# First products in a new order with filler matmuls, some normalizing work on GpSimd, and one layer norm cut in two

## The chip, the cores and the metric

The kernel is one program on one core of a Trainium2 chip. The metric is the device time of that core in microseconds (us), the median of several executions. Five engines run side by side, each through its own list of instructions in order: TensorE (PE in the profile, with its weight loads as PEld), VectorE (DVE), ScalarE (ACT), GpSimd (POOL) and SyncE (SP), which here only issues transfers. GpSimd issues transfers too, through a queue of its own. Engines wait for each other by semaphores.

## The reference

Two batches of 512 tokens with 512 features (x) go through three residual stages, each behind a layer norm without weights:

```python
x = x + xattn(layernorm(x), ctx, ctx, mask)   # 16 heads of 32; 8192 context tokens per batch
x = x + window_attn(layernorm(x))             # 16 heads, a window of 7 keys, latent projection
x = x + ffn(layernorm(x))                     # 16 experts, 128 tokens each, and a shared part
```

The first stage computes `q = ln(x) @ Wq.T + bq`, `k = ctx @ Wk.T + bk`, `v = ctx @ Wv.T + bv`, then `softmax(q k / sqrt(32)) v` with a mask over the 8192 keys, and `@ Wo.T + bo`. Everything is in float32, with the exception of small bfloat16 helpers (mask rows, subtracted maxima). The change touches the start of this stage and its end, where its projection meets the layer norm of the second stage.

## The kernel before

**Stage 1.** A unit is a batch and a group of four heads (8 units), a chunk is 512 context columns (16 per unit). The main loop goes over slots, one chunk per slot. In a slot the keys of the next chunk are projected (`project_k` and `keys_in`, products of L278), maxima of the scores are taken (`max_part`), and, 18 slots later, scores, exponentials and values of the same chunk are made. In the first 17 slots `max_part` runs four times per slot: four products with the mask row (L319), eight instructions of query times keys (L325), and two reductions on VectorE straight out of PSUM (L330). Its PSUM tiles come from a pool of three (`pairs`), two per call: the second tile of call 1 is the first tile of call 0 again, and has to wait until call 0's first reduction has read it. The queries of other head groups and of batch 1 are spread over these slots as single pieces (`later`), one behind each `max_part`. Batch 1's share of them is `query_norm` (its statistics) and four `query_in` (normalize 128 tokens, turn them on TensorE).

**Before the loop** stands `first_products`. SyncE issues the transfers in this order: token chunks 0 and 1 (128 tokens, 256 KB each, L70), the first 128 columns of Wq and of Wk (256 KB each, L168), the first context chunk in two halves (512 KB each, L484), token chunks 2 and 3, the four token chunks of batch 1 (1 MB, L63), the second context chunk (1 MB, L245), the rest of Wq (768 KB). GpSimd issues the mask and three bias vectors. `mask_rows` makes an additive mask (`mbias`, L209, on VectorE), spreads it over `junk` (L212, GpSimd), multiplies it with an identity to get the mask row of the first chunk (L218, copied by ScalarE, L222), and turns it whole (L226) so that GpSimd can write it to DRAM (L229, L233), from where later slots read their mask rows. `tokens_in` does statistics (L84, L85), square root (L88, ScalarE), reciprocal (L90), normalization (L94), four transposes (L502) and one copy back (L503, ScalarE) for one token chunk. After two of these come the first 256 queries (L192), then the keys of the first context chunk in halves (L278), then token chunks 2 and 3. The order on each engine is made by a scheduler that works with its own estimate of times; ScalarE's list there is: square roots of chunks 0 and 1, copy of chunk 0, square root of chunk 2, copy of chunk 1, mask row, square root of chunk 3, queries, keys.

**End of stage 1.** After the last slot eight `proj_residual` calls (L111 to L115) multiply by Wo and add to x, first four for batch 0, then four for batch 1. After the second one `finish_last` divides the last unit by its sums (reciprocal of 128x512, L458, then L462 and L463). After the fourth one `layernorm_stats` is called for batch 0, and behind each of the last four a chunk of batch 0 is normalized and turned (L606); the second stage begins with the products of L698, which wait for the copies of those four.

Of the kernel before, what the change touches and what calls it, by code (L numbers as in the profile page):

```python
# [19 lines left out]
P = 128  # L20
# [23 lines left out]
def perceiver_kernel(  # L44
# [45 lines left out]
        nc.vector.reciprocal(rs[:, these], sd[:, these])  # L90
        return mv, rs

    def normalized(dst, n, mv, rs):
        nc.vector.tensor_scalar(  # L94
            dst, x_sb[:, n, :], mv[:, n, 0:1], rs[:, n : n + 1], ALU.subtract, ALU.mult
        )

# [27 lines left out]
    with ExitStack() as es:  # L125
# [17 lines left out]
            return t  # L143

        mask_i = cp.tile([P, B, S2 // P], I32, name="mask_i")
        nc.gpsimd.dma_start(out=mask_i, in_=mask)
        bq_c = cp.tile([P, G], F32, name="bq_c")
        nc.gpsimd.dma_start(out=bq_c, in_=bq)
        bk_c = cp.tile([P, G], F32, name="bk_c")
        nc.gpsimd.dma_start(out=bk_c, in_=bk)  # L150
        bv_c = cp.tile([P, G], F32, name="bv_c")
        nc.gpsimd.dma_start(out=bv_c, in_=bv.rearrange("(g p) -> p g", p=P))
        ones32 = cp.tile([P, DK], F32, name="ones32")
        nc.vector.memset(ones32, 1.0)

# [6 lines left out]
        junk = cp.tile([P, KC], BF16, name="junk")  # L162
# [16 lines left out]

        def query_in(b, c):  # L180
            xn = tmp.tile([P, D], F32, tag="row", name="xn")
            normalized(xn, b * (NT // B) + c, *ln[b])
            transposed(xnT[b][:, :, ts(c, P)], xn, ps_q)

        pq = {}
# [20 lines left out]
        def mask_rows():  # L206


            nc.vector.tensor_scalar(mbias, mask_i, 0.0, -BIG, ALU.is_equal, ALU.mult)  # L209

            cols = junk.rearrange("p (c m) -> p c m", m=P)
            nc.gpsimd.tensor_scalar(  # L212
                cols, mbias[:, 0, 0 : KC // P].unsqueeze(2).to_broadcast([P, KC // P, P]),
                -1.0, None, ALU.mult,
            )
            tp = ps.tile([P, KC], F32, tag="ps", name="tpk")
            for c in range(KC // P):
                nc.tensor.matmul(  # L218
                    tp[:, ts(c, P)], lhsT=cols[:, c, :], rhs=ident_h, start=True, stop=True
                )  # L220
            mk_t[0] = mp.tile([P, KC], BF16, tag="mkh", name="mk", bufs=3)
            nc.scalar.copy(mk_t[0], tp)  # L222

            tp = ps.tile([P, B, P], F32, tag="ps", name="tpk")
            for b in range(B):
                nc.tensor.transpose(tp[0 : S2 // P, b, :], mbias[:, b, :], ident)  # L226
            mh = tmp.tile([S2 // P, P], BF16, name="mh")
            nc.vector.tensor_scalar(mh, tp[0 : S2 // P, 0, :], -1.0, None, ALU.mult)
            nc.gpsimd.dma_start(out=mrow_h, in_=mh)  # L229
# [246 lines left out]


        def first_products():
            load_cols(wq_sb, wq, slice(0, P))
            load_cols(wk_sb, wk, slice(0, P))  # L480
            ctx_t[0, 0] = ctxp.tile([P, DC, KC], F32, tag="ctx", name="ctx_t")
            for half in range(2):
                hs = ts(half, KC // 2)
                nc.sync.dma_start(  # L484
                    out=ctx_t[0, 0][:, :, hs],
                    in_=ctxT[0, :, hs].rearrange("(c p) s -> p c s", p=P),
                )
            load_chunks((2, 3))
            load_x(1)
            mask_rows()  # L490
            xnT[0] = pp.tile([P, DC, S], F32, tag="p", name="xnT")
            xn = pp.tile([P, NT // B, D], F32, tag="p", name="xn4")
            k_t[0] = kp.tile([P, KC], F32, tag="k", name="kt")

            def pair():
                return pairs.tile([P, 2, KC], F32, name="sx2")[:, 0, :]

            def tokens_in(c, tp):
                normalized(xn[:, c, :], c, *layernorm_stats(tmp, range(c, c + 1)))
                tp = tp.rearrange("p (n k) -> p n k", n=4)  # L500
                for i in range(4):
                    nc.tensor.transpose(tp[:, i, :], xn[:, c, ts(i, P)], ident)  # L502
                nc.scalar.copy(xnT[0][:, :, ts(c, P)], tp)  # L503
# [24 lines left out]
        def later_w(slot, dst, src, first):  # L528
# [1 line left out]
            load_cols(dst, src, slice(first, D))  # L530

        rest_in = {
            0: lambda: load_cols(wq_sb, wq, slice(P, D)),
            4: lambda: later_w(4, wk_sb, wk, P), 6: lambda: later_w(6, wv_sb, wv, 0),
        }
        wv_sb = cp.tile([P, DC, D], F32, name="wv_sb")
# [2 lines left out]
        for slot in range(NS + LAG):  # L539
            if slot == LAG:  # L540
                first_ps.close()
                ps = ps_q = ctx.enter_context(tc.tile_pool(name="a_ps", bufs=8, space=PSUM))
            if slot + 1 < NS + NKC:
                load(slot + 1)
            elif slot + 1 == NS + NKC:
                wo_sb = load_w(wo, ctxp, "ctx")
                wqkv_t = [load_w(wqkv[:, ts(i, D)], ctxp, "ctx") for i in range(3)]
            if slot + 1 < NS:
# [39 lines left out]
                    max_finish(u, i)  # L588


        turned_b0 = []
        for n in range(NT):
            if n == 1:
                values(*waiting)
            proj_residual(qT, wo_sb, None, n, ps, tmp)
            if n == 1:
                finish_last()
            m = n - NT // B
            if m == -1:
                ln_b0 = layernorm_stats(lnp, range(NT // B))  # L600
            if m >= 0:
                xn = tmp.tile([P, D], F32, tag="row", name="xn")
                normalized(xn, m, *ln_b0)
                tp = ps.tile([P, 4, P], F32, tag="ps", name="tp")
                for c in range(4):
                    nc.tensor.transpose(tp[:, c, :], xn[:, ts(c, P)], ident)  # L606
# [32 lines left out]
    with ExitStack() as es:  # L639
# [215 lines left out]
                )  # L855
            return pf

        lns, pairs = {"b0": ln_b0}, []
# [274 lines left out]
```

## Time and profile before

| what | value |
|---|---|
| median of 3 runs | 3671.01 us (3670.76 to 3671.19) |
| the profiled execution, its own time | 3670.19 us |
| its span in the trace | 3667.8 us |
| granted TensorE clock | 1.00 |
| TensorE busy | 3642.3 us, 99% of the span |
| VectorE, ScalarE, GpSimd busy | 2179.6, 1696.4, 2170.0 us |
| TensorE's first instruction | 7.41 us after the start of the span |
| first `max_part` begins | 25.65 us |
| end of stage 1's projections | about 2629 us |

A line of the timeline has the start in us, the busy time in us, the engine, the source line and operation, output<-inputs, shape and count; in square brackets is the idle time of the engine before it and what ended that. A line of the waits has the waiting engine and line, what it waited for, and the total, the count and the longest wait. The lines themselves stand in the prediction.

### The profile page before, as it was taken

The page shows a single profiled execution, that of the slowest core. Times are in us where ns is not written, and L with a number is a line of the kernel's source. Part 1 is how long each engine was busy: PE and PEld are TensorE (multiplying, and loading weights), DVE is VectorE, ACT ScalarE, POOL GpSimd, SP SyncE. Part 2 cuts the span into 40 slices and gives each one's busy share as a digit, 9 for nine tenths or more (in the row PEclk, how much of TensorE's full clock was granted, in tenths as well). Part 3 has the DMA queues.
Part 4 walks back from the last instruction along what each step waited for, and adds up shares of the span by engine and source line. Part 5 has one row for each costly group of instructions (what it writes and reads, how often), then busy time and mean ns, then how long its engine had stood idle before and what let it go on. Part 6 is the DMA issues. An engine that isn't in the chain of part 4 may idle for free.

```text
span 3667.8 us, 108951 instructions
## 1 busy us (share of the span) xinstructions
PE 3642.3 (99%) x47460; PEld 2057.9 (56%) x47460; DVE 2179.6 (59%) x5260; ACT 1696.4 (46%) x3417; POOL 2170.0 (59%) x653
## 2 busy tenths in 40 slices
PE   8999999999999999999999999999999999999999
PEld 4554555555455555545555555544455468888777
DVE  7976677677767766766776676789654711111111
ACT  2245555555555555555555555588554111111110
POOL 0059989998998999899899899921322000000000
PEclk9999999999999999999999999999999999999999
DMA  6322221221223443221222222122201068998886
GB/s 205 107 73 66 74 72 61 74 74 60 74 74 105 127 124 96 72 74 63 70 74 66 67 74 68 59 85 92 93 7 70 35 228 304 317 322 313 313 310 207
DMA packets 147757, 444.47 MB, mean 121 GB/s; under 512 B 9648, under 2 KB 14800, under 8 KB 121680
## 3 DMA queue, kind: packets, MB, share of 16 engines
q1 hardware_dynamic: 142224, 426.02, 34.5%
q0 software_dynamic: 5056, 11.50, 1.2%
q8 instruction: 372, 6.09, 0.7%
q14 instruction: 105, 0.86, 0.1%
HBM read 428.75 MB, written 8.73 MB: 119 GB/s over the span
## 4 chain that ended last, share of the span: by engine, by line
PE 97%; issue 1%; DMA 1%; POOL 1%; DVE 0%; ACT 0%; SPq 0%; POOLq 0%; DVEq 0%; ACTq 0%
PE av L428 14%; PE sx L338 13%; PE pk L278 12%; PE sc L404 12%; PE pv L296 12%; PE pf L1026 12%; PE py L1050 6%; PE pf L852 3%; PE sc L410 3%; PE pqkv L698 2%; PE sx L325 2%; PE po L111 2%; PE pso L973 1%; PE pq L192 1%; PE sx L319 1%
## 5 line engine op out<-in xcount | busy, mean ns | idle before, releaser
L452 POOL TENSOR_TENSOR acc<-acc,pt 128x2048 f32<-128x2048 f32 x437 | 1992.6, 4560 | 167.4 <-ACT pt L417 160.4
L343 DVE CUSTOM_DVE_ANT_0 junk<-sx,mk 128x512 bf16<-128x512 f32 x1776 | 1227.4, 691 | 627.7 <-PE sx L338 429.3
L417 ACT ACTIVATE pt<-sc,mbias 128x512 f32<-128x512 f32 x2016 | 1221.8, 689 | 786.6 <-PE sc L410 785.6
L296 PEld LDWEIGHTS pv<-wv_sb,ctx_t 128*32 128x32 f32 x16384 | 457.6, 110 | 176.1 <-DVE mst L343 103.2
L404 PE MATMUL sc<-qT,kt 32*128 32x512 f32 x4096 | 541.1, 594 | 0.0
L428 PE MATMUL av<-pt,vt 128*32 128x512 f32 x4032 | 537.6, 605 | 0.2 <-DVE mst L343 0.2
L338 PE MATMUL sx<-kt,qT 32*128 32x512 f32 x3552 | 507.7, 640 | 0.7 <-ACT vt L305 0.7
L296 PE MATMUL pv<-wv_sb,ctx_t 128*32 128x128 f32 x16384 | 500.1, 273 | 2.0 <-DVE avs L436 2.0
L278 PE MATMUL pk<-ctx_t,wk_sb 128*32 128x256 f32 (+1 forms) x9088 | 493.2, 357 | 0.0
L1026 PEld LDWEIGHTS pf<-xinT,wt 128*128 128x128 f32 x4096 | 461.0, 192 | 8.1 <-issue 7.2
L1026 PE MATMUL pf<-xinT,wt 128*128 128x128 f32 x4096 | 462.5, 275 | 0.7 <-ACT xinT L103 0.7
L278 PEld LDWEIGHTS pk<-ctx_t,wk_sb 128*32 128x32 f32 x9088 | 280.2, 109 | 296.6 <-DVE mst L343 101.6
L436 DVE TENSOR_TENSOR avs<-av,avs 128x512 f32<-128x512 f32 x504 | 345.0, 684 | 1.4 <-PE av L428 1.4
L404 PEld LDWEIGHTS sc<-qT,kt 32*128 32x128 f32 x4096 | 234.6, 184 | 187.7 <-issue 110.6
L1034 ACT ACTIVATE sg<-pf,bias_c 128x128 f32<-128x128 f32 x256 | 73.2, 369 | 542.9 <-PE pf L1026 542.9
L1055 POOL DMA_INDIRECT out_x<-y,idx x16 | 25.2, 1575 | 477.8 <-DVE y L1054 477.8
L428 PEld LDWEIGHTS av<-pt,vt 128*32 128x32 f32 x4032 | 79.7, 108 | 321.3 <-DVE mst L343 276.8
L1050 PE MATMUL py<-wt,eoT 128*128 128x512 f32 x512 | 222.4, 592 | 0.0
L282 ACT ACTIVATE kt<-pk,bk_c 128x256 f32<-128x256 f32 (+1 forms) x284 | 128.3, 452 | 202.1 <-PE pk L278 202.1
L1037 DVE SCALAR_TENSOR_TENSOR eoT<-pf,bias_c,sg 128x128 f32<-128x128 f32 x256 | 71.9, 344 | 243.7 <-PE pf L1026 243.7
L338 PEld LDWEIGHTS sx<-kt,qT 32*128 32x128 f32 x3552 | 139.5, 182 | 135.1 <-DVE mst L343 91.6
L410 PE MATMUL sc<-mT,neg 32*128 32x512 bf16 x2048 | 204.1, 374 | 0.0
(187 smaller groups left out, 2209.2 us busy)
## 6 DMA issues: line engine op xcount, KB each, us to landing
ctx_t<-in_ctxT SPq DMA_DIRECT2D x159, 1024.0 KB
wt<-in_gw SPq DMA_DIRECT2D x64, 1024.0 KB
wt<-in_up SPq DMA_DIRECT2D x64, 1024.0 KB
wt<-in_down SPq DMA_DIRECT2D x64, 1024.0 KB
mk<-mrow SPq DMA_DIRECT2D x111, 256.0 KB
wt<-in_sh_d SPq DMA_DIRECT2D x4, 1024.0 KB
y<-in_down_b SPq DMA_DIRECT2D x16, 256.0 KB
ctx<-in_wqkv SPq DMA_DIRECT2D x3, 1024.0 KB
```

The lines of the kernel that those rows point to most:

```text
L278: nc.tensor.matmul(pk[ts(h, DK), :], lhsT=wk_sb[:, c, ds(g * P + h * DK, DK)], rhs=ctx_t[slot, b][:, c, hs], start=(c == 0), stop=(c == DC ...
L296: nc.tensor.matmul(pv[ts(k, DK), i, :], lhsT=ctx_t[slot, b][:, c, ds((lo + i) * P + k * DK, DK)], rhs=wv_sb[:, c, ts(g, P)], start=(c == 0 ...
L338: nc.tensor.matmul(sm, lhsT=qT[r, g, ds(b * S + c * P, P)], rhs=k_t[s][r, :], start=True, stop=True)
L343: nc.vector.tensor_tensor_reduce(out=junk, in0=ss[h], in1=mk_t[s], scale=1.0, scalar=-3.0e38, op0=ALU.add, op1=ALU.max, accum_out=mst[u][: ...
L404: nc.tensor.matmul(sc, lhsT=k_t[s][r, ts(ch, P)], rhs=qT[r, g, ts(b, S)], start=True, stop=False)
L410: nc.tensor.matmul(ss[h], lhsT=neg[r, :], rhs=m_t[u][r, :], start=False, stop=True)
L417: nc.scalar.activation(pt[:, h, :], ss[h], AF.Exp, bias=mbias[:, b, cc : cc + 1], scale=SCALE)
L428: nc.tensor.matmul(av[ts(h, DK), :], lhsT=v_t[s][:, ch, ts(h, DK)], rhs=pt_t[s, ch][:, h, :], start=True, stop=True,)
L436: nc.vector.tensor_tensor(avs[u], av, avs[u], ALU.add)
L452: eng.tensor_tensor(acc[u], acc[u], pt_t[s, ch], ALU.add)
L1026: nc.tensor.matmul(pf[:, j, :], lhsT=wt[:, c, ts(j, P)], rhs=xinT[:, c, :], start=(c == 0), stop=(c == DC - 1),)
L1050: nc.tensor.matmul(py, lhsT=eoT[:, fq * 4 + c, :], rhs=wt[:, c, :], start=(fq == 0 and c == 0), stop=(fq == FQ - 1 and c == 3),)
```

## The change

At the start:

- a `junk` tile of 128x512 bfloat16 is cleared on VectorE, and 14 products of it with itself stand at the head of TensorE's list; nothing reads their result,
- SyncE's order becomes token chunks 0 and 1, Wk's first columns, first half of the context chunk, Wq's first columns, second half, token chunks 2 and 3 in one transfer, the second context chunk, batch 1's tokens, the rest of Wq; `load(1)` and the rest of Wq move there from slot 0,
- `load` of slots 2 and 3 gets a one-column GpSimd copy out of the turned tokens of chunk 1 into the context tile ahead of the transfer, so that the transfer waits for it,
- the first half of the keys is computed ahead of the first queries, the second half behind them,
- `mbias` is made on GpSimd, the bias of the queries is loaded ahead of the mask, and the turned mask gets a PSUM tile of the other pool,
- the normalization of batch 1's tokens in `query_in` moves from VectorE to GpSimd.

In the instruction lists that come out of this, ScalarE copies both chunk 0 and chunk 1 ahead of the square roots of chunks 2 and 3, and these two stand ahead of the copy of the mask row; on GpSimd the two one-column copies stand ahead of `mbias`; on VectorE batch 1's statistics stand ahead of the first reduction, as they did, without the two normalizations that followed them; TensorE has the turned mask and the mask row's products inside the first half of the keys.

At the end of stage 1 batch 0's layer norm is taken in two halves: statistics of chunks 0 and 1 after the second projection, with both normalized at once, and statistics of chunks 2 and 3 after the fourth. Chunk m+2 is normalized after chunk m has been turned. TensorE's order there is unchanged.

```diff
-    def normalized(dst, n, mv, rs):
-        nc.vector.tensor_scalar(
+    def normalized(dst, n, mv, rs, eng=nc.vector):
+        eng.tensor_scalar(
...
         mask_i = cp.tile([P, B, S2 // P], I32, name="mask_i")
-        nc.gpsimd.dma_start(out=mask_i, in_=mask)
         bq_c = cp.tile([P, G], F32, name="bq_c")
         nc.gpsimd.dma_start(out=bq_c, in_=bq)
+        nc.gpsimd.dma_start(out=mask_i, in_=mask)
...
+        junk = cp.tile([P, KC], BF16, name="junk")
+        nc.vector.memset(junk, 0.0)
+        tp = ps.tile([P, KC], F32, tag="ps", name="idle")
+        for _ in range(14):
+            nc.tensor.matmul(tp, lhsT=junk[:, 0:P], rhs=junk, start=True, stop=True)
...
-            normalized(xn, b * (NT // B) + c, *ln[b])
+            normalized(xn, b * (NT // B) + c, *ln[b], nc.gpsimd)
...
-            nc.vector.tensor_scalar(mbias, mask_i, 0.0, -BIG, ALU.is_equal, ALU.mult)
+            nc.gpsimd.tensor_scalar(mbias, mask_i, 0.0, -BIG, ALU.is_equal, ALU.mult)
...
-            tp = ps.tile([P, B, P], F32, tag="ps", name="tpk")
+            tp = ps_q.tile([P, B, P], F32, tag="ps", name="tpk")
...
+                if slot in (2, 3):
+                    nc.gpsimd.tensor_copy(t[:, 0, 0:1], xnT[0][:, 0, P : P + 1])
...
         def first_products():
-            load_cols(wq_sb, wq, slice(0, P))
             load_cols(wk_sb, wk, slice(0, P))
...
+                if half == 0:
+                    load_cols(wq_sb, wq, slice(0, P))
-            load_chunks((2, 3))
+            nc.sync.dma_start(
+                out=x_sb[:, 2:4, :], in_=x[2 * P : 4 * P, :].rearrange("(n p) d -> p n d", p=P)
+            )
+            load(1)
             load_x(1)
+            load_cols(wq_sb, wq, slice(P, D))
...
+            keys_in(0, pair()[:, 0 : KC // 2], ts(0, KC // 2))
             pq[0] = pair()[:, 0 : S // 2]
             for c in range(DC):
                 query(0, 0, 0, c, True)
-            for half in range(2):
-                keys_in(0, pair()[:, 0 : KC // 2], ts(half, KC // 2))
+            keys_in(0, pair()[:, 0 : KC // 2], ts(1, KC // 2))
...
             m = n - NT // B
             if m == -1:
-                ln_b0 = layernorm_stats(lnp, range(NT // B))
+                ln_b0.append(layernorm_stats(lnp, range(2, NT // B)))
+            if m == -3:
+                ln_b0.append(layernorm_stats(lnp, range(2)))
+                xns = [normalized_b0(0), normalized_b0(1)]
             if m >= 0:
-                xn = tmp.tile([P, D], F32, tag="row", name="xn")
-                normalized(xn, m, *ln_b0)
+                xn = xns[m]
+                if m < 2:
+                    xns.append(None)
...
+                if m < 2:
+                    xns[m + 2] = normalized_b0(m + 2)
```

More of the change, by code (lines that the diff above doesn't have):

```diff
@@ L161, in perceiver_kernel @@
         nc.vector.memset(mrep, 0.0)
-        junk = cp.tile([P, KC], BF16, name="junk")
         wk_sb = cp.tile([P, DC, D], F32, name="wk_sb")
@@ L532, in perceiver_kernel @@
         rest_in = {
-            0: lambda: load_cols(wq_sb, wq, slice(P, D)),
             4: lambda: later_w(4, wk_sb, wk, P), 6: lambda: later_w(6, wv_sb, wv, 0),
@@ L542, in perceiver_kernel @@
                 ps = ps_q = ctx.enter_context(tc.tile_pool(name="a_ps", bufs=8, space=PSUM))
-            if slot + 1 < NS + NKC:
+            if 0 < slot < NS + NKC - 1:
                 load(slot + 1)
-            elif slot + 1 == NS + NKC:
+            elif slot == NS + NKC - 1:
                 wo_sb = load_w(wo, ctxp, "ctx")
@@ L588, in perceiver_kernel, with normalized_b0 @@
                     max_finish(u, i)
-        turned_b0 = []
+        turned_b0, ln_b0 = [], []
+        def normalized_b0(m):
+            xn = tmp.tile([P, D], F32, tag="row", name="xn")
+            normalized(xn, m, *ln_b0[m // 2])
+            return xn
         for n in range(NT):
@@ L856, in shared_product @@
             return pf
-        lns, pairs = {"b0": ln_b0}, []
+        lns, pairs = {}, []
         at(2, norm, 1, "b1")
```

## The prediction

> **What bounds the kernel now.** I read the page's shares and chain first, then TensorE's waits, then the timeline at the two places that the change touches.
>
> ```profile
> PE 3642.3 (99%) x47460; PEld 2057.9 (56%) x47460; DVE 2179.6 (59%) x5260; ACT 1696.4 (46%) x3417; POOL 2170.0 (59%) x653
> ...
> PE 97%; issue 1%; DMA 1%; POOL 1%; DVE 0%; ACT 0%; SPq 0%; POOLq 0%; DVEq 0%; ACTq 0%
> ```
>
> TensorE is the bound for the whole span. A change of order can only win back its idle time, and the waits say where that is:
>
> ```profile
> engine line waited for: us in total, times, longest us
> PE sx L502 <- DVE rs L90: 7.4, 1, 7.4
> PE sx L192 <- ACT xnT L503: 4.2, 1, 4.2
> ...
> PE tp L606 <- DVE xn L94: 1.3, 1, 1.3
> ```
>
> The first two are the start, the third the end of stage 1. The timeline of the start shows what the 4.2 us are:
>
> ```profile
> 12.15 0.69 DVE L84 BATCH_NORM_STATS2 st<-x_sb 128x6 f32<-128x512 f32 x1 [4.10 <-DMA x_sb<-in_x]
> ...
> 13.16 0.29 ACT L88 ACTIVATE sd<-mv,eps 128x1 f32<-128x1 f32 x1 [4.04 <-DVE mv L85]
> 13.36 0.57 ACT L503 COPY xnT<-sx 128x512 f32<-128x512 f32 x1
> ...
> 13.98 1.06 PE L192 MATMUL sx<-xnT,wq_sb 128*32 128x256 f32 x2 [4.21 <-ACT xnT L503]
> ...
> 16.19 1.27 DVE L84 BATCH_NORM_STATS2 st<-x_sb 128x6 f32<-128x512 f32 x2
> ...
> 25.65 0.39 PE L319 MATMUL sx<-mk,neg 1*128 1x512 bf16 x4
> ...
> 26.95 2.36 DVE L330 TENSOR_REDUCE mst<-sx 128x2 f32<-128x1024 f32 x2 [3.50 <-PE sx L325]
> ...
> 28.71 0.40 PE L319 MATMUL sx<-mk,neg 1*128 1x512 bf16 x4
> ```
>
> The copy of token chunk 1 (13.36) stands on ScalarE behind the square root of chunk 2 (13.16), which waits for that chunk's transfer (landed 12.13 by the chain). So TensorE's first projection waits for tokens that it does not need. From 25.65 on it runs step after step: 25.65 and 28.71 are the first two `max_part`. What counts is how much earlier that sequence stands.
>
> **The start, step by step.** *Transfers.* Up to the landing of chunk 2 the queue moved 2.36 MB (0.26 for each token chunk and each column block, 0.52 for each context half). The new order moves the same 2.10 MB ahead of chunks 2 and 3, now one transfer, so both land where chunk 3 did: 12.13 plus 0.26 MB at 0.38 to 0.42 MB per us, 12.8. Then come the second context chunk and batch 1's tokens, 1.05 MB each, in the other order than before. I take the rate from two slices of the windows view (last column GB/s):
>
> ```profile
> 12.00:13.00 1.00, 0.00 (x0) 0.00 (x0) 0.81 (x3) 0.00 (x0) 0.00 (x0) 1.00 1.07 416
> ...
> 17.00:18.00 1.00, 1.00 (x16) 0.42 (x12) 1.00 (x4) 0.00 (x0) 0.91 (x2) 1.00 1.07 378
> ```
>
> All rows from 11 to 18 us lie between 375 and 416, mean 391. Batch 1's tokens thus land at 12.13 + (4.72 - 2.36) / 0.391 = 18.2 us (17.8 to 18.4 by the end rates). Before, their statistics could start at 16.19.
>
> *TensorE's own chain.* The VectorE wait for the mask (3.3 us, until 4.65) goes, but the statistics started at 4.80 right behind it, so at most some tenths are won: first transposes near 7.0 instead of 7.41. The 14 idle products start at about 1.2 us, behind a 0.27 us clearing (as the row of mrep), and take at most 14 x 0.43 = 6.0 us (at the slow rate, twice the 0.215 us per pass that eight L111 instructions in 3.44 us give). They end by 7.2, in time that was idle; their cost is nothing, at worst 0.2. The two copies now follow the transposes, the second ends near 9.0. Keys start at 8.4 (half chunk landed by 8.2, from the same sum). On GpSimd two one-column copies (0.19 each, by L526), `mbias` and `junk` (1.53, L212) follow 9.0. `mbias` on GpSimd is not in the trace: between 0.23 (L209 on VectorE) and 1.53 (four times its columns); I take 0.5, a third of the latter with some fixed part. `junk` is ready at 11.6. TensorE stops for it with 13 of 16 key products done. Then mask 0.4, 3 keys 0.3, queries 1.75 and keys 1.75 (32 instructions at 0.054 each): 15.8.
>
> *ScalarE's chain* is later: statistics of two chunks 1.6 from 12.8, two square roots 0.5, mask row 0.59, keys 0.47, queries 0.47, keys 0.47, copy of chunk 2 0.59: 17.5 with gaps. Only then chunk 3's transposes may use the one PSUM tile, and from there to the first `max_part` it is 1.16 (24.49 to 25.65 before): 18.65, that is 7.0 us earlier.
>
> *VectorE's chain* is later still. Its list has batch 1's statistics ahead of the first reduction. From 18.2: 2.9 for four statistics (16.19 to 19.07 before), 0.65 for square root, reciprocal and hand-overs, 1.22 for the first reduction, 0.05: 23.0. Until then the second tile of step 1 is taken, and TensorE, which would be there at 18.65 + 3.2 = 21.85, waits 1.15 us. Before it was there at 28.87. The gain of the start is 28.87 - 23.0 = 5.9 us. Later steps do not queue: two reductions are 2.4, a step 3.1.
>
> *Moved at no cost.* Loads of slots 2 and 3 wait for the one-column copies (done near 9.4), but stand behind the mask row's load, which waits for GpSimd's DRAM write (20.38 before, about 19.0 now: 14.9 + 4.1 us to landing). The slot-2 chunk then lands near 24 and is wanted near 30. The rest of Wq lands near 20.5, wanted near 26; if a transfer were 4 us late the cover would be gone. The second context chunk lands near 15.5, wanted at 16.6. GpSimd's four normalizations are bounded by L462 (1.29) and L557 (3.14); I take L463, the only TENSOR_SCALAR of that size, 1.84. Behind the first two stand the copies that hold Wk's and Wv's rest, run at 59.7 and 80.8, so nothing is late. Each of the last two has more than one 3.2 us step between the transposes that free its buffer and its own. The turned mask's other PSUM tile, the bias order and `load`'s condition change no time on the path.
>
> The clock is the other thing the idle products touch. In the groups view the first 32 L192 instructions took 634 ns, the other 480 took 379, and the step up came near 20.2 us, 6.2 after 13.98. [...]
>
> **The end of stage 1.** Before:
>
> ```profile
> 2605.16 10.57 PE L111 MATMUL po<-ctx,qT 128*128 128x512 f32 x24
> ...
> 2605.91 3.35 DVE L458 RECIPROCAL rl<-rl 128x512 f32<-128x512 f32 x1
> ...
> 2614.07 0.30 ACT L88 ACTIVATE sd<-mv,eps 128x4 f32<-128x4 f32 x1 [6.89 <-DVE mv L85]
> ...
> 2617.03 0.66 PE L606 MATMUL tp<-ident,xn 128*128 128x128 f32 x4 [1.31 <-DVE xn L94]
> ```
>
> In halves, chunk 0's square root can run at 2607.2, and its normalization (0.52) behind the 3.35 us reciprocal, one addition and one product on VectorE: done at 2611.3, four us ahead of 2615.7, when TensorE is there. The 1.31 us go. The last unit's bias (L463) slips by 0.5 to 2611.9, wanted near 2614.8. Chunk 2 waits for chunk 0's transposes, has 8 us. The 0.67 us wait of L698 for the last copy stays. Bounds: 0 to 1.31; I take all of it.
>
> **Sum.** 5.9 + 1.3 = 7.2 us off 3670.19, the profiled execution's time: 3663.0. That execution lies 0.8 under the median of the runs, so on the median's scale 3663.8. What a measurement can tell from no change is about 0.2%, 7.3 us; the bound lies at 3663.7.
>
> **Rivals.** *Batch 1's tokens are no bound.* If they land before 17.05, ScalarE's chain rules and the gain is 7.0 + 1.3 = 8.3: 3662.7. For it: TensorE really is free there; against it: no rate in the rows is high enough.
>
> *The array stays slow.* If products on zeros leave the clock down, 13 keys end at 11.2, the rest of the block at about 18.5, `max_part` starts near 20.9 and step 1's second tile is wanted at 24.1: 4.8 + 1.3, 3664.9. For it: the slow rows of before; against it: 6 us of dense work.
>
> *GpSimd's normalizations hold VectorE up* (the other side). The first two run next to the first reductions, the others next to slot 7 and 8. No reduction of L330 has GpSimd beside it before. For it: GpSimd's own 128x512 TENSOR_TENSOR took 1.29 alone and 3.14 (L557) beside VectorE's additions. Against it: L343 on VectorE takes 0.69 with and without GpSimd's additions. If each holds a reduction for its whole length, 4 x 1.29 to 4 x 3.14 less 1.6 slack in the later steps: 3.6 to 11.0 lost, 3667.4 to 3674.8. Slower than before from 2.2 us each, by more than 0.2% from 4.0. [...]
>
> *The halves bring nothing*, if the wait at L606 only moves: 3665.1.
>
> **Numbers.** Forecast 0.50 (landing at 17.6 to 18.6: 3663.2 to 3664.3, of which 0.20 under the bound); first rival 0.20; second 0.14; third 0.10 (0.07 within, 0.03 slower); fourth 0.03; something unseen and slower 0.03. Faster 0.40, within 0.54, slower 0.06. The range 3662.3 to 3667.4 leaves out the fast edge of the first rival and most of the third.
>
> **What would show it.** The first `max_part` near 18.6 with one wait of about 1.1 us in the second one, for the first L330; statistics of batch 1 starting at 18.2; no 1.31 at L606; L192's first group near 379 ns. A L330 longer than 1.22 us or a wait of TensorE in slots 7 and 8 means the third rival; a first `max_part` after 20 the second.

## The result and the profile after

| | time, us | runs from | to |
|---|---|---|---|
| before, on the same chip | 3671.15 | 3669.28 | 3672.19 |
| after | 3663.28 | 3660.80 | 3669.77 |
| predicted | 3663.8 | 3662.3 | 3667.4 (the range) |

The ratio is 0.9981, with a 95% interval of 0.9975 to 0.9987: the kernel is 7.9 us faster, on the edge of the 0.2% that the prediction called the limit of the measurement. The profiled execution took 3663.66 us, with a span of 3661.3 us, 6.5 us less than the profiled one of before. Its mean granted clock is 0.999, not 1.00, and that thousandth turns out to matter.

TensorE is the bound as it was. From the page of the kernel after, busy times and the chain:

```profile
PE 3645.3 (100%) x47474; PEld 2059.2 (56%) x47474; DVE 2177.7 (59%) x5257; ACT 1696.5 (46%) x3418; POOL 2178.9 (60%) x660
...
PE 97%; issue 1%; DMA 1%; POOL 1%; DVE 0%; SPq 0%; ACT 0%; POOLq 0%; DVEq 0%; ACTq 0%
```

The waits of TensorE after (total us, times, longest us). The waits of 7.4, 4.2 and 1.3 us of before are gone. In their place are 1.6 for the first half of the context chunk and 1.4 plus some tenths for the first reductions. The wait of 2.0 for `avs` (VectorE's sum of the attention's values), which both kernels have late in the main loop, now leads the list:

```profile
PE pv L303 <- DVE avs L443: 2.0, 1, 2.0
PE sx L326 <- DVE mst L337: 1.8, 2, 1.4
PE sx L285 <- DMA ctx_t<-in_ctxT: 1.6, 1, 1.6
...
PE pqkv L721 <- ACT xnT L891: 0.7, 1, 0.7
```

The start, from the timeline after (start, busy, engine, line and operation, in brackets the idle time ahead and what ended it). Line numbers are shifted: L326 is the mask product of `max_part`, L332 its query times keys, L337 its reduction, L514 the transposes, L285 the keys.

```profile
3.68 0.69 DVE L84 BATCH_NORM_STATS2 st<-x_sb 128x6 f32<-128x512 f32 x1 [2.06 <-DMA x_sb<-in_x]
...
6.72 1.04 PE L514 MATMUL sx<-ident,xn 128*128 128x128 f32 x8
...
9.33 1.89 PE L285 MATMUL sx<-ctx_t,wk_sb 128*32 128x256 f32 x26 [1.57 <-DMA ctx_t<-in_ctxT]
...
12.98 1.29 DVE L84 BATCH_NORM_STATS2 st<-x_sb 128x6 f32<-128x512 f32 x2 [6.17 <-DMA x_sb<-in_x]
...
18.27 0.39 PE L326 MATMUL sx<-mk,neg 1*128 1x512 bf16 x4
...
18.43 1.29 DVE L84 BATCH_NORM_STATS2 st<-x_sb 128x6 f32<-128x512 f32 x2 [2.34 <-DMA x_sb<-in_x]
...
21.85 4.79 DVE L337 TENSOR_REDUCE mst<-sx 128x2 f32<-128x1024 f32 x4
22.05 4.14 POOL L94 TENSOR_SCALAR xn<-x_sb,mv,rs 128x512 f32<-128x512 f32 x2 [5.25 <-DVE rs L90]
...
23.10 0.39 PE L326 MATMUL sx<-mk,neg 1*128 1x512 bf16 x2 [1.38 <-DVE mst L337]
...
26.16 0.40 PE L326 MATMUL sx<-mk,neg 1*128 1x512 bf16 x4
```

The row at 18.27 is the first `max_part`, 23.10 is the wait in the second, and 26.16 is the third. In the trace of before, the third is

```profile
31.77 0.39 PE L319 MATMUL sx<-mk,neg 1*128 1x512 bf16 x4
```

so TensorE stands 5.61 us earlier. The two normalizations on GpSimd (22.05) run beside the four reductions (21.85), and these take 4.79 / 4 = 1.20 us each; two of before took 2.36, 1.18 each.

The end of stage 1 after, also from the timeline:

```profile
2602.72 0.30 ACT L88 ACTIVATE sd<-mv,eps 128x2 f32<-128x2 f32 x1
...
2605.91 0.54 DVE L94 TENSOR_SCALAR xn<-x_sb,mv,rs 128x512 f32<-128x512 f32 x1
...
2611.08 0.60 PE L627 MATMUL tp<-ident,xn 128*128 128x128 f32 x4
```

The first chunk is normalized at 2605.91, five us ahead of its transposes, and L627 (the transposes there) has no wait. The stretch from the first projection to the second stage's first window score, in the timelines of before and of after:

```profile
2595.90 3.70 PE L111 MATMUL po<-ctx,qT 128*128 128x512 f32 x8
...
2642.43 0.64 PE L758 MATMUL sw<-ext,q_t 32*103 32x109 f32 x16
```
```profile
2591.43 3.70 PE L111 MATMUL po<-ctx,qT 128*128 128x512 f32 x8
...
2636.42 0.64 PE L781 MATMUL sw<-ext,q_t 32*103 32x109 f32 x16
```

It was 46.53 us and is 44.99 now: 1.54 us. The wait of 0.67 for the last copy stays as 0.68.

Start and end make 5.61 + 1.54 = 7.15 us, and the span is 6.5 us shorter. In between, time was lost. It lies behind the 2.0 us wait. The timeline of TensorE after, at that place:

```profile
2387.90 1.17 PE L303 MATMUL pv<-wv_sb,ctx_t 128*32 128x128 f32 x32 [1.99 <-DVE avs L443]
...
2389.22 2.09 PE L411 MATMUL sc<-qT,kt 32*128 32x512 f32 x8
```

and the windows of 1 us there (the number ahead of the last two columns is the granted clock):

```profile
2388.00:2389.00 1.00, 1.00 (x40) 0.98 (x40) 1.00 (x1) 0.00 (x0) 0.00 (x0) 0.88 0.00 0
2389.00:2390.00 1.00, 1.00 (x16) 0.54 (x10) 1.00 (x2) 0.54 (x2) 0.00 (x0) 0.50 0.06 16
...
2392.00:2393.00 1.00, 1.00 (x17) 0.34 (x12) 0.84 (x1) 1.00 (x3) 0.00 (x0) 0.92 0.00 0
```

The clock falls to one half at 2388.76 (0.24 us of that window at half speed make 0.88) and comes back at 2392.16: 3.4 us at half speed, up to 1.7 us lost. Eight score products took 2.09 us instead of 1.14. From the end of the wait to the first projection it is 203.53 us (2387.90 to 2591.43), and 201.95 before (2393.95 to 2595.90): 1.58 lost. The rest of the 6.5 us is about half a microsecond won in the main loop ahead of the wait and as much behind TensorE's last product, neither of them forecast. The profiled execution of before has the same wait, from the timeline:

```profile
2393.95 1.08 PE L296 MATMUL pv<-wv_sb,ctx_t 128*32 128x128 f32 x32 [2.02 <-DVE avs L436]
```

and no such stretch; its windows from 2394 to 2401 all show 1.00. So the same wait was followed by half clock in one traced execution and not in the other. That made the second question of the experiments: besides where the gain comes from, what of the times is this.

### The profile page after: what moved, and what is told of

Its sections match the earlier page's. It is cut to its first block, busy times and chain, and to the rows that moved or that the text cites. A ratio compares the mean times of both kernels' runs of the same rounds, so it can differ in the third digit from the quotient of the medians.

```text
span 3661.3 us, 108992 instructions
## 1 busy us (share of the span) xinstructions
PE 3645.3 (100%) x47474; PEld 2059.2 (56%) x47474; DVE 2177.7 (59%) x5257; ACT 1696.5 (46%) x3418; POOL 2178.9 (60%) x660
## 4 chain that ended last, share of the span: by engine, by line
PE 97%; issue 1%; DMA 1%; POOL 1%; DVE 0%; SPq 0%; ACT 0%; POOLq 0%; DVEq 0%; ACTq 0%
PE av L435 14%; PE sx L345 13%; PE sc L411 12%; PE pk L285 12%; PE pv L303 12%; PE pf L1049 12%; PE py L1073 6%; PE pf L875 3%; PE sc L417 3%; PE pqkv L721 2%; PE sx L332 2%; PE po L111 2%; PE pso L996 1%; PE pq L197 1%; PE sx L326 1%
## 5 line engine op out<-in xcount | busy, mean ns | idle before, releaser
L285 PE MATMUL pk<-ctx_t,wk_sb 128*32 128x256 f32 (+1 forms) x9088 | 493.2, 357 | 0.0
L285 PEld LDWEIGHTS pk<-ctx_t,wk_sb 128*32 128x32 f32 x9088 | 280.4, 109 | 296.2 <-DVE mst L350 101.4
```

The source lines that it names most:

```text
L285: nc.tensor.matmul(pk[ts(h, DK), :], lhsT=wk_sb[:, c, ds(g * P + h * DK, DK)], rhs=ctx_t[slot, b][:, c, hs], start=(c == 0), stop=(c == DC ...
```

## The experiments

Each run stands beside runs of the kernel before on the same chip. Times are medians; "after" is 3663.28, or 3663.2 as measured again. The runs are from several chips, on which the kernel before has medians of 3671.15 (after), 3670.77 (runs 1 to 4), 3670.58 (5 to 8) and 3670.45 (9 to 12), so distances of run 5 and the later ones from after are uncertain by some 0.7 us.

**1. The changed kernel again**, as the base of the first three parts.

> The changed kernel once more, unaltered, as the yardstick for the others on the same chip, and for the spread of its times (3660.8 to 3669.8 against 3669.3 to 3672.2 of the kernel before). Theory A, half-clock windows: the granted clock falls to a half for about 3.5 us where TensorE had to wait 1.4 us or more (in the traced execution behind the 2.0 us wait at 2386 us), 1.75 us lost each time; then times go with the mean granted clock, 0.001 being some 3 us, executions at 1.000 lie at 3660.8 to 3662.1, and the trace shows any loss only behind such a wait. Theory B, transfers that land at different times: then the times vary at a granted clock of 1.000 as well, and the first max_part moves between executions.

3663.2 (3660.99 to 3666.98), ratio 0.998 (0.9971 to 0.9989). Sorted by their mean granted clock, the 31 times of both measurements fall apart: 11 runs at 1.000 have a mean of 3661.4 (3660.8 to 3662.1), 15 at 0.999 one of 3664.0, four at 0.998 one of 3666.7, one at 0.997 took 3669.8. One stretch of 3.4 us at half speed lowers the mean by 3.4 x 0.5 / 3660 = 0.0005 and loses some 1.7 us, so that 0.999 stands for one or two stretches. (The means are rounded and take in up to 3 us at half clock at the end of the traces, behind the last product: the traced execution of run 5 has one stretch and reads 1.000.) The steps of 2.5 to 3.1 us between the groups fit that: the spread of 9 us is mostly the half clock.

**2. The halves of the layer norm alone**, in the kernel before:

```diff
...
             if m == -1:
-                ln_b0 = layernorm_stats(lnp, range(NT // B))
+                ln_b0.append(layernorm_stats(lnp, range(2, NT // B)))
+            if m == -3:
+                ln_b0.append(layernorm_stats(lnp, range(2)))
+                xns = [normalized_b0(0), normalized_b0(1)]
...
```

> The kernel before with only the layer norm in halves at the end of stage 1. My theory: the 1.31 us wait at the first transposes of batch 0 goes and nothing takes its place, 3669.8 on the scale of the median of before, start unchanged (first max_part at 25.65). Rival, the wait only moves (to L698 or to the last unit's bias): 3671.1. Second rival, the four layer norm pieces push later VectorE work of that stage: above 3671.5.

3669.32 against 3670.77: 1.45 us. The ratio, 0.9996 (0.9987 to 1.0006), holds no change too; the trace settles it: the wait for `xn` is gone, and the stretch from the first projection to the first window score is 45.00 us, as after. The same trace has two half-clock stretches. One of 3.4 us follows the 2.0 us wait, at 2392.97. The other is in stage 2, behind a wait of only 0.93 us, from the timeline and the windows:

```profile
2785.04 0.39 PE L823 MATMUL pow<-pT,vt 109*32 109x103 f32 x8 [0.93 <-DVE pT L813]
```
```profile
2785.00:2790.00 5.00, 4.96 (x47) 3.10 (x48) 3.67 (x29) 4.51 (x27) 2.01 (x3) 0.55 0.01 3
2790.00:2795.00 5.00, 5.00 (x20) 2.37 (x19) 1.25 (x3) 1.90 (x11) 1.60 (x2) 0.77 0.00 0
```

4.5 and 2.3 us at half speed make 6.8 us, twice the 3.4 of above.

**3. Without the idle products**, whose result nothing reads:

```diff
-        tp = ps.tile([P, KC], F32, tag="ps", name="idle")
-        for _ in range(14):
-            nc.tensor.matmul(tp, lhsT=junk[:, 0:P], rhs=junk, start=True, stop=True)
```

> The changed kernel without the 14 idle products (the clearing of junk stays). My theory: the array starts at half speed, 8 transposes take 1.9 us instead of 1.0, the first key products run at 0.107 us each instead of 0.054, the first max_part starts 1.5 to 2.6 us later (19.8 to 20.9 instead of 18.3), and as TensorE waits there for the first reduction until 23.1 anyway, only 0 to 1.3 us of it reach the end: 3663.3 to 3664.6 if the changed kernel is at 3663.3. Rival, the idle products carry much of the gain: 3665.5 or more. Rival, they only use up clock windows and cost time: below 3662.8.

3662.39 (3660.52 to 3663.35), ratio 0.9977 (0.9968 to 0.9986): nothing lost, if anything 0.9 us won, which by the number alone would be the rival in which the products cost time. The array is slow at the start without them (eight transposes 1.94 us, not 1.04), and the first `max_part` begins at 20.13 instead of 18.27. But the third one begins at 26.41 against 26.16. The 1.9 us by which TensorE is ahead end in the wait for the first reductions. Run 11 measures this again without the half clock.

**4. Batch 1's tokens loaded in slots 2 to 5**, one chunk per slot, to take their transfer away from the start:

```diff
             load(1)
-            load_x(1)
...
+        def later_x(slot):
+            n = NT // B + slot - 2
+            held(slot, x_sb[:, n, 0:1])
+            load_chunks((n,))
...
```

> The changed kernel with batch 1's four token chunks loaded one per slot in slots 2 to 5, each behind a one-column copy of an earlier maximum, so that their statistics stand behind the first reductions instead of ahead of them. My theory (the landing of batch 1's tokens at 18.4 us, through VectorE's list, sets the second max_part): first max_part stays at 18.3, the 1.4 us wait there goes with the 0.3 before it, step 2 starts near 24.5 instead of 26.2, 1.7 us less in all (3661.6 if the changed kernel is at 3663.3), less up to 0.5 for statistics among the later reductions. Rival, something else holds the first reduction (ScalarE, or the mask row): the wait stays and the time is that of the changed kernel. Second rival, the statistics delay later reductions by as much as is won: same time, with waits of TensorE for L337 spread over slots 2 to 6.

3689.45 (3687.49 to 3690.1), ratio 1.005 (1.0037 to 1.0064): 26 us slower than after, which neither theory said. The part that it was made for does show: the second `max_part` has no wait, the first reduction begins at 19.81, the third `max_part` at 24.63, 1.5 us earlier than after. But VectorE's list has each chunk's statistics ahead of later reductions, and now they wait for a transfer that starts late. From the timeline:

```profile
37.01 0.69 DVE L84 BATCH_NORM_STATS2 st<-x_sb 128x6 f32<-128x512 f32 x1 [5.55 <-DMA x_sb<-in_x]
...
38.89 0.61 PE L326 MATMUL sx<-mk,neg 1*128 1x512 bf16 x2 [5.43 <-DVE mst L337]
...
38.89 2.31 PE L332 MATMUL sx<-kt,qT 32*128 32x512 f32 x8
```

TensorE waits 16.4 us in five such waits, 14.6 more than after, and four of them bring a stretch of 6.8 us at half clock (behind 38.89 it is 2.31 us for what takes 1.03), up to 13.7 us lost. A load moved away without its reader only moves the wait, and makes it longer. Run 5 moves the reader instead.

**5. Batch 1's statistics behind early reductions**, its tokens loaded early:

```diff
-    def layernorm_stats(pool, tokens=range(NT)):
+    def layernorm_stats(pool, tokens=range(NT), behind=None):
...
+            if behind is not None:
+                behind(st[:, 0:1], n)
             nc.vector.bn_stats(out=st, in_=x_sb[:, n, :])
...
+                lambda dst, n: nc.gpsimd.tensor_copy(
+                    dst, mst[0][:, 3, 3, n - NT // B + 1 : n - NT // B + 2]
+                ),
...
```

> The changed kernel, with batch 1's tokens still loaded early, but each of its four statistics put behind an early maximum on VectorE by a one-column GpSimd copy of that maximum into the statistics tile. It parts what my forecast called the bound of the start (VectorE's list holds the first reduction back behind statistics that wait for the transfer) from the transfer itself. If the forecast's mechanism is right: first reduction at 19.8 instead of 21.85, no wait in the second max_part, step 2 at 24.6 instead of 26.16, 1.5 us off 3663.3: 3661.8. Rival: the four statistics (0.65 us each, 0.15 to 0.3 for the aggregate) now stand between reductions, 3.2 us of VectorE work in steps that TensorE ends in 2.6 us; with 0.6 us lost in each of four steps the gain is given back: 3663.3 to 3664.2.

3664.69 (3663.3 to 3667.77), ratio 0.9983 (0.9974 to 0.9992): 1.4 us slower than after. The rival was right, and more than it said was given back. From the timeline:

```profile
24.01 0.40 PE L333 MATMUL sx<-mk,neg 1*128 1x512 bf16 x4
...
41.65 0.69 DVE L86 BATCH_NORM_STATS2 st<-x_sb 128x6 f32<-128x512 f32 x1 [0.28 <-POOL st L186]
...
43.72 0.39 PE L333 MATMUL sx<-mk,neg 1*128 1x512 bf16 x2 [0.36 <-DVE mst L344]
```

The third `max_part` begins at 24.01 instead of 26.16, the first reduction at 19.19, and the second `max_part` does not wait: the statistics ahead of the first reduction were what held the start. But in later slots two reductions are 2.36 us in a step of 2.63, and every statistics, aggregate and hand-over puts VectorE behind. From the third `max_part` to the 33rd it was 80.01 us after and is 83.91 here: 3.9 lost for 2.15 won.

**6. One addition handed over earlier.** The 2.0 us wait comes where the additions to `acc` (the sums of the exponentials) switch from GpSimd to VectorE: VectorE's first one waits for GpSimd's last one, and `avs` stands behind it. Here the last addition of the step before the switch goes to VectorE:

```diff
-                eng = nc.gpsimd if s + LAG <= NS else nc.vector
+                eng = nc.gpsimd if s + LAG < NS or s + LAG == NS and ch < 3 else nc.vector
```

> The changed kernel, with the additions of the last step before the switch from GpSimd to VectorE moved to VectorE for its fourth chunk, so that VectorE's first addition does not wait for GpSimd's last one. It asks what the 2.0 us wait of TensorE at 2385.9 and the half-clock stretch behind it are worth. Theory A (the spread of the times is half-clock stretches behind waits): the wait of 2.0 goes, with it the 1.75 us of the stretch in those executions that have it, so 2.0 to 3.7 us less at the median, 3659.6 to 3661.3, and a narrower spread than the 3660.8 to 3669.8 of the changed kernel. Theory B (the spread comes from landing times at the start): 2.0 us less at the most and the same spread. Rival: the wait only moves to the next finished unit on VectorE, and the time stays at 3663.

3659.38 (3659.02 to 3661.83), ratio 0.997 (0.9958 to 0.9981): 3.9 us faster than after, 0.2 below the range expected, and 11.2 faster than before on the same chip. The wait is gone, and nothing of the kind replaces it; the waits of TensorE begin with

```profile
PE sx L326 <- DVE mst L337: 2.1, 2, 1.6
PE sx L285 <- DMA ctx_t<-in_ctxT: 2.0, 1, 2.0
```

The runs at full mean clock of after had 3661.4, so some 2.0 us are the wait and 1.9 the half clock in most of its executions. The expected narrow spread is there: six of seven runs within 1.3 us.

**7. The mask and batch 1's normalizations back on VectorE:**

```diff
-            normalized(xn, b * (NT // B) + c, *ln[b], nc.gpsimd)
+            normalized(xn, b * (NT // B) + c, *ln[b])
...
-            nc.gpsimd.tensor_scalar(mbias, mask_i, 0.0, -BIG, ALU.is_equal, ALU.mult)
+            nc.vector.tensor_scalar(mbias, mask_i, 0.0, -BIG, ALU.is_equal, ALU.mult)
```

> The changed kernel with the additive mask and batch 1's normalizations back on VectorE: the move to GpSimd undone, the new order of transfers and products kept. By my forecast's steps: VectorE waits for the mask again before the first statistics (3.68 to 4.8 at most, hidden by the wait for the context half chunk, which lands at 9.3), and two normalizations of 0.5 us go in front of or between the first reductions. If they go in front, TensorE's wait in the second max_part grows from 1.4 to 2.4: 3664.3. If behind: 3663.3. Rival (GpSimd beside the reductions costs VectorE time, my third rival): faster than 3662.5.

3665.06 (3664.1 to 3668.59), ratio 0.9986 (0.9977 to 0.9995): 1.8 slower than after, 0.8 more than the dearest of the two expectations. The reason is one that I had not thought of. The scheduler put the mask behind the statistics of chunk 2 on VectorE:

```profile
13.05 0.70 DVE L84 BATCH_NORM_STATS2 st<-x_sb 128x6 f32<-128x512 f32 x1 [6.28 <-DMA x_sb<-in_x]
13.66 0.21 DVE L214 TENSOR_SCALAR mbias<-mask_i 128x128 f32<-128x128 int32 x1
...
13.92 0.41 PE L231 MATMUL tpk<-ident,mbias 128*64 128x128 f32 x2 [2.73 <-DVE mbias L214]
```

so TensorE waits 2.7 us for it, 0.8 more for `junk`, and the first `max_part` begins at 23.87. The clock is at one half from 15.11 to 18.52 behind the first of these, up to 1.7 us of it. The third `max_part` begins 3.9 us later than after in these traces; this execution has no half clock behind the 2.0 us wait, which wins some of that back. What the mask on GpSimd is worth is its place in a list that waits for nothing, not VectorE's 0.21 us.

**8. Runs 5 and 6 together.**

> Both of the former edits together (statistics behind the first maxima, and the additions handed over one chunk earlier), as the version that may beat both kernels. If the two add: 3663.3 less 1.5 less 2.0 to 3.7, so 3658.1 to 3659.8. If the statistics give their gain back: 3659.6 to 3661.3. If the second wait only moves: 3661.8.

3661.58 (3661.18 to 3663.11), ratio 0.9975 (0.9965 to 0.9985): 2.2 slower than run 6 alone. So the statistics behind the reductions lose their gain here too; the median is 0.3 above the case in which they only give it back.

**9 and 10. Run 6 again, and its edit in the kernel before**, to see the change with this wait out of both:

> The changed kernel with the fourth chunk's addition handed to VectorE one step earlier, a second time, as the base for the three runs beside it: without the 2.0 us wait the times should stay close together (3659.0 to 3661.8 the first time), so that tenths can be told. Expected 3659.4. If the narrow spread of the first time was the chip's, the times spread to 3663 or more again.

> The kernel before, with that same edit alone. It has the same 2.0 us wait, and I claim that the wait and the half clock behind it are no part of the change: then it falls from 3670.6 by 2.0, and by 1 to 1.7 more if its usual execution has the half-clock stretch too: 3666.9 to 3668.6, and what the change itself brings, with this noise out of both, is 3667.8 less 3659.4: 8.4, or at least 7.5. Rival: only the changed kernel suffers from the half clock; then this one falls by 2.0 at the most and the difference to the base is over 9.2.

3659.75 (3658.64 to 3661.52), ratio 0.9971 (0.996 to 0.9982), and 3667.15 (3665.41 to 3669.87), ratio 0.9991 (0.9982 to 1.0). The narrow spread of run 6 came again. The edit takes 3.5 us off the kernel after (2.8 to 3.6 in runs 6 and 9, by the distances from before on each chip) and 3.3 off the one before (3670.45 there): the wait and its half clock are in both alike and no part of the change. The kernel before does not get a narrower spread by it, 4.5 us in 11 runs against 4.1 in 25. The change itself is then worth 3667.15 - 3659.75 = 7.4 us. I had expected 8.4, at least 7.5.

The trace of run 10 also shows that the kernel before does not start the same every time. Its first `max_part` begins at 24.05, in run 2 at 23.93, in the profile that the prediction was made from at 25.65. Its products reached full speed some three us earlier: the first 27 L192 took 2.50 us, not 3.21.

**11. Run 6 without the idle products** (the diff of run 3):

> The base without the 14 products whose result nothing reads. Theory A (TensorE only runs ahead into the waits for the transfers; the 0.9 us by which the changed kernel was faster without them was its half-clock executions): within 0.4 of the base, 3659.2 to 3659.8. My forecast's second rival (the array stays slow, 1.1 lost): 3660.5. Theory C (they do harm): 3658.5.

3659.68 (3658.82 to 3660.38), ratio 0.997 (0.9959 to 0.9981), beside 3659.75 with them: nothing, theory A. From its timeline:

```profile
18.78 1.29 DVE L84 BATCH_NORM_STATS2 st<-x_sb 128x6 f32<-128x512 f32 x2 [2.47 <-DMA x_sb<-in_x]
...
20.06 0.39 PE L323 MATMUL sx<-mk,neg 1*128 1x512 bf16 x4
...
26.51 0.39 PE L323 MATMUL sx<-mk,neg 1*128 1x512 bf16 x4
```

Six traces have the statistics of batch 1 ahead of the first reduction and nothing added there. They say what sets the start:

| kernel | first `max_part` | statistics of batch 1 start | third `max_part` | difference |
|---|---|---|---|---|
| run 1 | 17.95 | 17.97 | 25.70 | 7.73 |
| after | 18.27 | 18.43 | 26.16 | 7.73 |
| run 6 | 18.40 | 18.81 | 26.54 | 7.73 |
| run 9 | 18.27 | 19.12 | 26.85 | 7.73 |
| run 3, no idle products | 20.13 | 18.68 | 26.41 | 7.73 |
| run 11, no idle products | 20.06 | 18.78 | 26.51 | 7.73 |

Whether TensorE is at its first `max_part` at 18 or at 20, the third follows 7.73 us after the landing of batch 1's tokens. That landing moves by 1.15 us between executions.

**12. Run 6 with the normalizations back on VectorE**, the mask left on GpSimd (the first pair of lines of the diff of run 7):

> The base with batch 1's four normalizations back on VectorE, the mask left on GpSimd: the part of the earlier run with both on VectorE that was not told apart. Two normalizations of 0.5 us then stand in front of the first reduction: TensorE's wait in the second max_part 1.4 to 2.4 us, 3660.4; the other two take 0.5 us each between reductions of steps with 0.27 us to spare, up to 0.5 more: 3660.9. If GpSimd beside reductions cost VectorE something after all (my third rival), the base would be the slower one: 3658.9.

3662.41 (3660.17 to 3667.04), ratio 0.998 (0.9971 to 0.9989): 2.7 slower than run 9, and 1.5 over the dearest of the times expected. From the timeline and the windows:

```profile
24.48 0.39 PE L326 MATMUL sx<-mk,neg 1*128 1x512 bf16 x2 [2.38 <-DVE mst L337]
...
25.66 1.83 PE L285 MATMUL pk<-ctx_t,wk_sb 128*32 128x128 f32 x32
```
```profile
25.50:26.00 0.50, 0.50 (x15) 0.34 (x15) 0.40 (x2) 0.00 (x0) 0.00 (x0) 0.83 1.03 248
26.00:26.50 0.50, 0.50 (x17) 0.50 (x12) 0.50 (x1) 0.00 (x0) 0.00 (x0) 0.50 1.02 248
...
29.00:29.50 0.50, 0.50 (x8) 0.11 (x4) 0.00 (x0) 0.25 (x1) 0.00 (x0) 0.76 0.97 365
```

The wait ends 5.73 us after the statistics' start (18.75), in run 9 it ended 4.68 after (19.12 to 23.80): 1.05 for two normalizations, as expected. The rest is not in any list: behind the wait of 2.38 the clock is at one half from 25.83 to 29.24, 3.4 us, and the third `max_part` is another 1.6 later. By the clocks of its runs this is usual: seven of 11 are below 1.000, in run 9 one of seven.

## Why the prediction was right, point by point

*Batch 1's tokens as the bound.* The step that carries the prediction held, and is shown in six traces: tokens, four statistics, square root, first reduction. Predicted landing 18.2, measured 18.43; end of TensorE's wait 23.0 and 23.10; its length 1.15 and 1.38. At the end of the wait the gain was 28.87 - 23.10 = 5.77, for 5.9. One step on it was 5.61: the eight L332 behind the split call took 1.24 us instead of 1.03. The first rival, tokens that are no bound, falls with the table under run 11.

*TensorE's own chain.* The terms were wrong on the way and it did not matter. The keys began at 9.33, not 8.4: the half context chunk landed 1.1 us later than my sum of bytes had it. The transposes were at 6.72 (7.0 predicted), and at full speed, 1.04 us for eight. `mbias` on GpSimd took 0.68 us, 0.5 predicted; `junk` was ready at 11.2, 11.6 predicted; chunks 2 and 3 landed at 12.98 (12.8). The first 32 query products took 380 ns each, 379 predicted. The first `max_part` came at 18.27, for 18.65.

*The idle products cost nothing*: right, run 11 has 3659.68 without and 3659.75 with them. The second rival had a slow array as a loss of 1.1 us; the array is slow without the products (first `max_part` 1.8 us later) and nothing of it is lost. That rival put the first `max_part` at 20.9 and the need for the second tile at 24.1, behind the landing's bound. Measured, it begins at 20.06 and needs the tile 3.2 later, at 23.3, when the first reduction (18.78 + 4.68) is just about to be done: the wait for the tokens swallows the delay whole.

*GpSimd's normalizations* took 2.07 us each, 1.84 predicted, inside the bounds of 1.29 and 3.14. (The 1.84 is a mean of six at 1.57 and one at 3.48.) The third rival, VectorE held up by them, falls twice: the reductions beside them took 1.20 us, and run 12 without them is slower. Four reductions took 4.79 us beside GpSimd, and 4.78 in run 5 at 42.48 us, where GpSimd had nothing to do. What I had not priced was the alternative: with the normalizations on VectorE the wait is 1.05 us longer, and in run 12 that wait, 2.38 us, was followed by 3.4 us at half clock.

*The end of stage 1* brought 1.54 us in the trace and 1.45 at the median of run 2, for 1.31 predicted. The wait shown was 1.31; the other 0.2 us are at the same place: after, the transposes begin 0.17 ahead of the end that the trace gives the products before them (2611.08, and 2600.68 + 10.57 = 2611.25), and take 0.60 instead of 0.66. The fourth rival falls.

*The sum.* 7.2 predicted, 7.15 in the two places, 7.9 at the medians, 7.4 with the late wait taken out of both kernels. That these agree within a microsecond is in part luck: the profiled execution of before started 1.6 us later than two others of its start, and had no half-clock stretch, where by their mean clocks most of its executions have one (22 of 27 at 0.999 on one chip, 17 of 27 and 20 of 25 on two more). These two nearly cancel. One profiled execution is a sample, and the prediction took its start for the start. No run has the new order of transfers and products alone: that it carries the gain of the start is argued, from what is left when the halves (run 2), the idle products (run 11) and the work on GpSimd (runs 7 and 12) are told apart.

*The clock.* The step that failed: the sum has no term for a clock that falls behind a wait. That it would stay at full speed was the author's estimate, which no run had shown: the kernel before already had a gap of 2.02 us, the wait for `avs`, which the prediction's list of waits leaves out, and its clock of 1.00 behind it is that of one execution. Here the clock fell behind waits of 0.93 (run 2), 1.99 (after), 2.38 (run 12) and 2.73 us (run 7), and behind longer ones in run 4. In the 14 traces there are six stretches of 3.41 us at half speed and five of 6.83. The kernel after has waits of 1.6, 1.4 and 2.0 us, and most executions show a lowered mean clock (20 of 31 are below 1.000); in the traced one only the wait of 2.0 was followed.

The kept traces say much of when a wait is followed. In the trace of after the granted clock changes at 2388.75, at 2392.17 and, behind the last products, at 3658.51: the half clock lasts 3.41 us, and the last change comes 1266.34 us later, 371 times 3.4133. Lay a row of windows of that length through the changes of each trace, and a wait falls into one or across a border. Two windows of after, and the two of before that hold its wait (set by the fall of its clock at 3665.63, 374 times 3.4133 us after 2389.06):

```profile
2385.34:2388.75 3.41, 1.42 (x40) 0.85 (x36) 3.41 (x3) 2.07 (x4) 0.00 (x0) 1.00 0.00 0
2388.75:2392.17 3.42, 3.42 (x34) 1.14 (x28) 3.42 (x3) 0.90 (x3) 0.00 (x0) 0.50 0.02 5
```
```profile
2389.06:2392.47 3.41, 2.87 (x44) 0.90 (x32) 1.47 (x1) 2.83 (x7) 1.91 (x1) 1.00 0.00 0
2392.47:2395.89 3.42, 1.94 (x48) 1.44 (x52) 3.42 (x3) 1.51 (x4) 0.00 (x0) 1.00 0.02 5
```

The first number behind the length is TensorE's busy time. Its wait lay whole in one window after (1.99 us idle), and the next window was at half clock; before it lay across a border (0.54 and 1.48 idle), and nothing followed. Eight traces have this wait: in after and runs 1, 2 and 5 a window held at least 1.98 us of it and the half clock followed, in before and runs 3, 4 and 7 none held more than 1.61 and it did not. The waits of the start fit: run 12 has 2.07 idle in one window and run 7 has 2.45, followed; run 9's wait of 2.08 is split into 0.91 and 1.17, and run 4 has a window with 1.67, not followed.

Not settled: what counts in a window beside idle time. The wait of 0.93 us in stage 2 is in all 14 traces and was followed in one, and a window with 1.99 us idle, where run 5's last products end, was not followed. Why some stretches last two windows is open too. Not tried: an order of transfers that lands batch 1's tokens before 17 us, which might give up to 1.5 us more, the difference between 26.16 and the third `max_part` of run 4 at 24.63.

## What to carry to other kernels

When an engine is given something to do while it waits, ask which wait ends last: products that had TensorE fast when its work came (eight transposes in 1.04 us, not 1.94) moved its first `max_part` by 1.8 us and the end by nothing, because a list on another engine stood behind a transfer. An instruction that waits for a transfer costs what stands behind it in its list, so look at the place of the reader before moving the load; moved to a place without slack, it costs more than in an idle one (run 4: 26 us). And on this kernel, whose main engine is busy 99% of the time, a single wait of 2.0 us was worth removing for more than its own length: 2.8 to 3.9 us (runs 6 and 9).

## What the runs showed of the hardware that was not expected

TensorE's granted clock fell to one half behind single waits of 0.93 us (run 2) to 5.4 us (run 4), in some executions and not in others, for 3.4 us or 6.8 us at a time, at up to 1.7 us lost for each 3.4. In the windows of 3.41 us that its changes mark off in each trace, in the start and the main loop, once full speed had come, it fell after each of the ten with 1.98 us idle or more, and after none with 1.67 or less; a window with 1.99 idle at run 5's last products was not followed. Taking one wait of 2.0 us out (runs 6 and 9) was worth 2.8 to 3.9 us at the median of the changed kernel, by the chip that it is compared on, and 3.3 of the one before. It brought the changed kernel's spread from 9 us in 31 executions down to 3 in 14. GpSimd's 128x512 normalizations took 2.07 us beside VectorE's reductions, four times VectorE's 0.5, and the reductions were as long as without them (four in 4.79 us, and in 4.78 in run 5). The version of run 6, 3659.4 to 3659.8 us, is faster than both kernels: ratio 0.997 to before, with an interval of 0.9958 to 0.9981.
